# Moving one basis step behind the sums of the next layer, with VectorE's units and one norm reordered around it

## The chip, the cores and the metric

The kernel runs on one core of one Trainium2 chip. The metric is the device time of one execution in microseconds (us), the median of several runs. Where a single execution is looked at in detail it is the one that the hardware profiler recorded; its times count from the start of its span.

## The reference

A graph network of four layers works on 512 nodes with 512 features each (float32), with 16,896 edges. Each layer takes `h = relu(layernorm(x))` and adds its result to `x`.

- Layer 0 is attention with 8 heads over the edges, then a feed-forward part with two layer norms.
- Layer 1 is a linear map with PReLU, and then twice the same round: `x + segment_sum(x[src], dst)`, a product with `conv_W1`, PReLU, a product with `conv_W2`, a batch norm over the nodes (per feature), relu.
- Layer 2 is a graph convolution: `out = segment_sum(norm * (h @ W)[src], dst) + b`, then a leaky relu.
- Layer 3 is two relational convolutions. Each needs two matrices `w[r] = sum_b att[r, b] * basis[b]` from 30 bases of 512x512, for two relations and for each of the two convolutions; the basis matrices are most of what is read from memory (60 MB).

```
w = jnp.einsum('rb,bio->rio', att, basis)          # layer 3, twice
agg = jax.ops.segment_sum(x[src], dst, num_segments=n); h = x + agg   # layer 1, twice
h = _prelu(h @ conv_W1[l].T + conv_b1[l], conv_a[l]); h = h @ conv_W2[l].T + conv_b2[l]
h = (h - mean) * rsqrt(var + eps) * bn_gamma[l] + bn_beta[l]; x = relu(h)
```

## The kernel before

Nodes and features are tiles of 128 rows; `T` is 4, so a 512x512 matrix is a tile of 128 partitions by 4 by 512. The segment sums are dense products: the edges are first counted into a 512x512 matrix (`Cl` for layers 1 and 2, `Bc` for the two relations of layer 3), and a sum over edges is then a product with the counts.

The bases of layer 3 are worked into the two matrices all through the earlier layers, so that their reading from memory lies beside other work. Part of them goes over TensorE (PE) and part over VectorE:

- A **basis step** (`basis_step`) is one PE entry: four matmuls (L242) that multiply a load of up to 15 bases, cut to a few rows of each, with a small matrix of coefficients, into the PSUM bank `bas`. Two steps (in the second convolution's part three, the last with a smaller load in two pieces, L202) fill one bank; then ScalarE copies the bank to `sums` (L248) and issues a DMA to memory (L249). There is one `bas` bank, so the next bank's first step waits for that copy.
- A **unit** (`accumulate`) is a VectorE entry's quarter: one instruction (L272) that adds a coefficient times half a basis to one of the two `wrel` matrices. `advance(more, n)` issues n units; four units finish one basis.

The string `USES` gives the order in which the loads of both kinds follow each other: "P" for a basis step, "V" for a basis that VectorE uses. All loads go through one pool of four buffers (`bpool`) and are issued by SP in this order, so a load starts when an earlier entry has set its buffer free; taking an entry asks for the one three places on. Entries are numbered from 0 in the text; entry 36 is the first one behind the first batch norm's products.

The weight matrices (`w`, L160) come by DMAs that POOL issues, from a pool of three buffers; one is asked for ahead, and is issued when PE has done its last product with the buffer's former content.

The stage around the change is layer 1 and the start of layer 2. For each of the two rounds `l`:

1. the sums: 32 matmuls (L324 with four banks `acc`, in round 0 L947) into four banks; ScalarE copies banks 0 and 2 (L983) and VectorE banks 1 and 3 (L981) to `aT`;
2. four products with `conv_W1` (L324), each with a bias on ScalarE (L996) and PReLU on VectorE (L998, L999), and two units behind each;
3. four products with `conv_W2`, a bias on ScalarE (L1009), then for each of the four groups of features: the moments on VectorE (L348, L349), the root on ScalarE (L845), four small instructions on VectorE (L847 to L851), and the norm with relu on ScalarE (L852). `settle` then transposes a group on PE (L337); in round 0 it is rounded into two parts (L858, L859), in round 1 it is added to `x` (L861);
4. basis steps between the last groups.

Layer 2 starts with the moments of the four tiles of `x`, a root on ScalarE (`root`, L1039), three small instructions on VectorE (`scale`, L1042 to L1044), and the norm on ScalarE (`normed_to`, L1047), once rounded into `xn[0]` and once in full into `h`; VectorE writes the difference into `xn[1]` (L1059, L1065). Then PE runs the sums of layer 2 (`gather`, L947), with the products `gate_rows` (L809) ahead of them to fill PE's time.

Each engine runs its instructions in the order in which they stand. Most of that order is the order of the program, but a scheduler may move instructions; those that are wrapped in `on` (or in `keep_in_program_order`) stay in their order among each other. Where an `if` on a value stands around the sums (`exactly`), both branches are built and one is run.

Of the kernel before, what the change touches and what calls it, by code (L numbers as in the profile page):

```python
# [17 lines left out]
P = 128  # L18
# [12 lines left out]
RB = 4  # L31
STEPS = 2
BANKS = 8
USES = "P" * 26 + "VPVVVPPVVVPPPPVVVVPPPPPPPVVVVVVVVVVVV"
FEW = 4095
LESS = 2.0 ** -12
GW = 32
# [37 lines left out]
def gnn_kernel(ctx: ExitStack, tc: tile.TileContext, out: bass.AP, a: dict):  # L75
# [18 lines left out]
    def bank(tag):  # L94
        if tag == "sc":
            return pair()[:, 0].rearrange("p i n -> p (i n)")
        return psum[-1].tile([P, 512], F32, tag=tag, name=tag, bufs={"ao": 2, "ps": 1, "acc": 4, "pr": 2, "pg": 1}[tag])

    def ps():
        turn[1] += 1  # L100
        return bank(turn[0][turn[1] % len(turn[0])])

    def big(tag):
        return work.tile([P, T, 512], F32, tag=tag, name="big" + tag)
# [101 lines left out]
    def whole_load(l, b):  # L206
        def load():
            t = bpool.tile([P, T, 512], F32, tag="basis", name="basis")
            nc.sync.dma_start(t, nat(a[f"basis{l + 1}"][b]))
            return t  # L210
        return load
# [3 lines left out]
    ve = iter([whole_load(l, b) for l in range(2) for b in range(ONPE[l], NB)])  # L215
    bases = Stream([next(pe if u == "P" else ve) for u in USES], 0)
    bases.ahead = AHEAD
# [7 lines left out]
    def basis_step(n=1, keep=lambda ins: ins, held=None):  # L225
        for _ in range(n):
            if len(done) == len(loads):
                return
            l, n, g = loads[len(done)]
            done.append(n)  # L230
            assert USES[bases.at] == "P"
            t = bases.take()
            if g == 0:
                sums[:] = [pbas.tile([P, 512], F32, tag="bas", name="bas")]
            if g < STEPS:
                k, at = FULL * NQ, 32 - 2 * NQ * (g + 1)
                lhsT = wide[l][:k, at:at + 32]
            else:
                k = STEPS * HALF_OF * NQ
                lhsT = wide2[:k, :]  # L240
            for j in range(RB):
                tc.keep_in_program_order(nc.tensor.matmul(  # L242
                    sums[0][32 * j:32 * j + 32, :], lhsT=lhsT,
                    rhs=t[:k, j, :], start=(g == 0), stop=(g == STEPS + l - 1)))
            if g == STEPS + l - 1:
                def leave(n=n, bank=sums[0]):
                    o = spool.tile([P, 512], F32, tag="sums", name="sums")
                    keep(nc.scalar.copy(o, bank))  # L248
                    nc.scalar.dma_start(summed[l][n], o)  # L249

                if held is None:
                    leave()
                else:
                    held.append(leave)
# [9 lines left out]
    def accumulate(l, to):  # L264

        for b in range(ONPE[l], NB):
            assert USES[bases.at] == "V"
            t = bases.take()
            for r in range(2):
                at = AT1 + 2 * NB * l + NB * r + b  # L270
                for i in range(0, T, 2):
                    on(nc.vector.scalar_tensor_tensor(to[r][:, i:i + 2, :], t[:, i:i + 2, :], scal[:, at:at + 1],  # L272
                                                      to[r][:, i:i + 2, :], op0=ALU.mult, op1=ALU.add))
                    yield
# [47 lines left out]
    def product(p, pairs):  # L322
        for i, (lhsT, rhs) in enumerate(pairs):
            nc.tensor.matmul(p, lhsT=lhsT, rhs=rhs, start=(i == 0), stop=(i == len(pairs) - 1))  # L324

    def ts(i):
        return slice(i * P, (i + 1) * P)

    def on(ins):

        return tc.keep_in_program_order(ins)
# [11 lines left out]
    def stat(name, n=1):  # L343
        return small.tile([P, n], F32, name=name, bufs=3)

    def moments(mv, v, keep=lambda ins: ins):
        st = stat("st", 6)
        keep(nc.vector.bn_stats(st, v))  # L348
        keep(nc.vector.bn_aggr(mv, st))  # L349
# [340 lines left out]
    def advance(gen, n=1):  # L690
        for _ in range(n):
            next(gen, None)
# [109 lines left out]
    more = accumulate(0, wrel)  # L802
# [23 lines left out]
    def parts(hi, lo):  # L826

        return [late.tile([P, T, 512], F32R, tag=t, name=t) if t in "FG" else
                work.tile([P, T, 512], F32R, tag=t, name="big" + t) for t in (hi, lo)]
# [4 lines left out]
    def exactly(emit):  # L834

        with tc.If(made["few"] > 0) as branch:
            emit(lambda v: v, 1)
        with branch.Else():
            emit(f32, 0)

    def normed(l, h2T, m, mv):

        at = T * l + m
        sd = stat("sd")
        nc.scalar.activation(sd, mv[:, 1:2], AF.Sqrt, bias=eps)  # L845
        sg = stat("sg")
        nc.vector.reciprocal(sg, sd)  # L847
        nc.vector.tensor_mul(sg, sg, cols[:, GAM + at:GAM + at + 1])
        off = stat("off")
        nc.vector.tensor_mul(off, mv[:, 0:1], sg)  # L850
        nc.vector.tensor_sub(off, cols[:, BET + at:BET + at + 1], off)  # L851
        on(nc.scalar.activation(h2T[:, m, :], h2T[:, m, :], AF.Relu, bias=off, scale=sg))  # L852
# [84 lines left out]
    xn = parts("C", "F")  # L937
# [29 lines left out]
    for l in range(2):  # L967

        aT = big("E")
        if l:  # L970
            acc = [bank("acc") for _ in range(T)]

            def emit(f, c):
                for m in range(T):
                    product(acc[m], [(f(xn[i][:, k, ts(m)]), Clx[c][:, k, :]) for k in range(T) for i in range(2)])
            exactly(emit)
            advance(more, 3)
        for m in range(T):
            p = acc[m]
            if m % 2:  # L980
                on(nc.vector.tensor_copy(aT[:, m, :], p))  # L981
            else:
                on(nc.scalar.copy(aT[:, m, :], p))  # L983
        if l == 0:
            basis_step(1, on)
            advance(more, 4)
        else:
            advance(more, 2)
        w = weights.take()
        h1T = big("B")  # L990
        for m in range(T):
            p = ps()
            product(p, [(w[:, k, ts(m)], aT[:, k, :]) for k in range(T)])
            at = CB1 + T * l + m
            z = small.tile([P, 512], F32, name="z")
            nc.scalar.activation(z, p, AF.Identity, bias=cols[:, at:at + 1])  # L996
            u = small.tile([P, 512], F32, name="u")
            nc.vector.tensor_scalar(u, z, 0.0, scal[:, CA + l:CA + l + 1], op0=ALU.min, op1=ALU.mult)  # L998
            nc.vector.scalar_tensor_tensor(h1T[:, m, :], z, 0.0, u, op0=ALU.max, op1=ALU.add)  # L999
            advance(more, 2)  # L1000
        w = weights.take()
        h2T = big("D")
        if l == 0:
            xn = parts("A", "G")
        for m in range(T):
            p = ps()
            product(p, [(w[:, k, ts(m)], h1T[:, k, :]) for k in range(T)])
            at = CB2 + T * l + m
            on(nc.scalar.activation(h2T[:, m, :], p, AF.Identity, bias=cols[:, at:at + 1]))  # L1009
            if m:  # L1010
                normed(l, h2T, m - 1, moment)
            moment = stat("mv", 2)
            moments(moment, h2T[:, m, :])
            if m > 1:
                settle(l, h2T, m - 2, xn)
            if l and m < 3:
                advance(more)
        basis_step(1)
        normed(l, h2T, 3, moment)
        settle(l, h2T, 2, xn)  # L1020
        basis_step(3 - l)
        settle(l, h2T, 3, xn)
        if l:
            held = []
            gates = gate_rows(1, [apart.bitcast(F32).rearrange("p t n -> p (t n)")[:, N * r:N * r + N] for r in range(2)])
            next(gates)
            basis_step(1, on, held)
# [5 lines left out]
    xn = parts("C", "F")  # L1033
# [4 lines left out]
    def root(t):  # L1038
        on(nc.scalar.activation(sd4[:, t:t + 1], mv[:, t, 1:2], AF.Sqrt, bias=eps))  # L1039
# [6 lines left out]
    def normed_to(to, t):  # L1046
        on(nc.scalar.activation(to[:, t, :], x[:, t, :], AF.Relu, bias=nm[:, t:t + 1], scale=by[:, t:t + 1]))  # L1047

    for t in range(T):
        moments(mv[:, t, :], x[:, t, :], on)  # L1050
        root(t)
        if t:
            scale(t - 1)
        if t > 1:
            normed_to(xn[0], t - 2)
    scale(3)
    for t in (0, 1):
        normed_to(h, t)
# [180 lines left out]
```

## Time and profile before

| what | value |
|---|---|
| median of 3 runs | 510.31 us (509.25 to 510.54) |
| profiled execution: its own time | 511.07 us |
| profiled execution: span | 509.1 us |
| PE busy | 483.9 us (95%), 2014 instructions |
| VectorE (DVE) busy | 399.3 us (78%) |
| ScalarE (ACT) busy | 195.6 us (38%) |
| POOL busy | 37.9 us (7%) |
| chain that ended last | PE 67%, DVE 18%, ACT 8%, issue 2%, DMA 2% |
| read from memory | 88.38 MB, 184 GB/s over the span |

The profiled execution's own time is its span and 1.97 us around it. "PE" is the matmuls and "PEld" the loading of their stationary operands, which overlaps them. In a timeline each row has the start, the time that it takes, the engine, the line of the source, the operation, what it writes and reads, the count, and in brackets how long the engine stood idle before it and what ended that. In the chain each row has start, time, engine, tile, line and count; it is followed back from the last instruction. A float32 matmul shows as two matmul records, so a product of four has "x8". The DMA rows have the queue (q0 is POOL's, q1 is SP's, q10 is ScalarE's), packets, MB, and the share of the 16 DMA engines' time. In the table by stretch each engine has its busy time and count, then come the granted clock of PE, the DMA share and GB/s.

### The profile page before, as it was taken

To read this page: it belongs to the slowest core of one execution; us is meant where nothing else is said; L and a number is where in the kernel's file an instruction comes from. 1 tells how busy PE (TensorE), PEld (TensorE's weight loads), DVE (VectorE), ACT (ScalarE), POOL (GpSimd) and SP (SyncE) were. 2 spreads that over 40 slices of the span, in tenths; PEclk is the share of its full clock that TensorE was granted. 3 is DMA by queue.
4 is the path that set the end of the run, shared out by engine and by line. 5 is a ranking of instruction groups with operands and counts; after the bars stand their busy time and mean duration, and the time that the engine had idled before them with its cause. 6 is when DMAs were issued, how large, how long until landed. Compare 5 with 4: busy or idle time off the path is not lost.

```text
span 509.1 us, 5732 instructions
## 1 busy us (share of the span) xinstructions
PE 483.9 (95%) x2014; PEld 249.0 (49%) x2014; DVE 399.3 (78%) x748; ACT 195.6 (38%) x318; POOL 37.9 (7%) x81
## 2 busy tenths in 40 slices
PE   3999999999999999999999999899899999999996
PEld 2333333255564547864445444444654584446642
DVE  6847487879999779999885974797659999998611
ACT  4876779724444213223332134115624610133000
POOL 7000000100000021310040000000010100000000
PEclk9999999999999999999999999999899999999999
DMA  8999768998968499586552695866944965420011
GB/s 243 282 248 250 180 175 194 230 258 198 216 160 198 105 226 293 220 227 191 210 182 84 149 238 195 305 184 156 269 143 154 287 190 217 165 82 3 0 42 41
DMA packets 42951, 94.06 MB, mean 185 GB/s; under 512 B 2113, under 2 KB 2567, under 8 KB 42919
## 3 DMA queue, kind: packets, MB, share of 16 engines
q1 hardware_dynamic: 34682, 68.17, 49.7%
q0 software_dynamic: 5712, 21.07, 13.9%
q10 hardware_dynamic: 2525, 4.39, 2.6%
q8 instruction: 20, 0.33, 0.3%
q14 instruction: 12, 0.10, 0.1%
HBM read 88.38 MB, written 5.24 MB: 184 GB/s over the span
## 4 chain that ended last, share of the span: by engine, by line
PE 67%; DVE 18%; ACT 8%; issue 2%; DMA 2%; ACTq 0%; DVEq 0%
PE pr L324 19%; PE acc L1145 11%; PE pg L324 10%; PE acc L1111 5%; PE ps L484 4%; PE acc L947 3%; PE bas L242 3%; DVE sc L648 3%; ACT sc L649 3%; ACT hs L553 3%; DVE sc L666 3%; PE ao L562 2%; DMA basis<-in_basis 2%; DVE half L642 2%; PE ps L497 2%
## 5 line engine op out<-in xcount | busy, mean ns | idle before, releaser
L272 DVE SCALAR_TENSOR_TENSOR wrel<-basis,scal,wrel 128x1024 f32<-128x1024 f32 x60 | 74.0, 1281 | 3.9 <-DMA basis<-in_basis 3.9
L553 ACT ACTIVATE hs<-iot,key 128x512 f16<-128x512 f16 x75 | 48.8, 711 | 5.5 <-PE ao L562 4.7
L549 DVE TENSOR_SCALAR hd<-iot,key 128x32 f16<-128x32 f16 (+1 forms) x132 | 33.3, 293 | 15.4 <-PE ao L562 15.2
L242 PE MATMUL bas<-basis,wide 120*32 120x512 f32 (+1 forms) x320 | 43.5, 600 | 0.7 <-ACT sums L248 0.7
L272 DVE SCALAR_TENSOR_TENSOR w<-basis,scal,w 128x1024 f32<-128x1024 f32 x32 | 39.3, 1276 | 0.0
L562 PE MATMUL ao<-hs,hd 128*32 128x512 f16 x204 | 25.8, 397 | 2.8 <-ACT hs L553 2.6
L649 ACT ACTIVATE sc<-sc 128x2048 f32<-128x2048 f32 (+1 forms) x10 | 15.7, 1568 | 32.6 <-DVE sc L648 32.6
L484 PE MATMUL ps<-bigB,w 128*128 128x512 f32 x56 | 27.2, 615 | 0.9 <-ACT bigD L487 0.6
L324 PE MATMUL pr<-bigE,w 128*128 128x512 f32 x48 | 21.6, 596 | 1.4 <-DVE bigE L981 1.4
L1195 DVE TENSOR_TENSOR u<-acc,x 128x512 f32<-128x512 f32 (+1 forms) x5 | 2.8, 582 | 23.5 <-PE acc L1145 23.5
L324 PE MATMUL pr<-bigD,w 128*128 128x256 f32 x88 | 20.2, 380 | 0.0
L555 DVE TENSOR_SCALAR hs<-iot,key 128x512 f16<-128x512 f16 x57 | 19.2, 345 | 0.0
L648 DVE TENSOR_TENSOR sc<-sc,half 128x2048 f32<-128x2048 f32 (+1 forms) x10 | 18.6, 1862 | 0.2
L666 DVE TENSOR_TENSOR sc<-sc,rec 128x2048 f32<-128x2048 f32 x8 | 18.3, 2284 | 0.0
L633 PE MATMUL psc<-bigC,bigD 64*128 64x256 f32 x128 | 18.2, 402 | 0.0
L324 PEld LDWEIGHTS pr<-bigD,w 128*128 128x128 f32 x88 | 16.6, 190 | 3.0 <-ACT bigE L891 0.8
L356 ACT ACTIVATE sd<-mv,eps 128x1 f32<-128x1 f32 x16 | 4.7, 296 | 34.4 <-DVE mv L349 33.4
L562 PEld LDWEIGHTS <-hd 128*32 128x32 f16 x204 | 6.1, 94 | 24.2 <-issue 15.4
L324 PE MATMUL pr<-w,bigE 128*128 128x512 f32 x40 | 17.8, 592 | 0.0
L484 PEld LDWEIGHTS ps<-bigB,w 128*128 128x128 f32 x56 | 9.7, 189 | 14.9 <-issue 11.1
L664 DVE RECIPROCAL rec<-ps 128x256 f32<-128x256 f32 x8 | 14.0, 1752 | 3.7 <-PE ps L660 3.7
L635 ACT COPY sc<-psc 128x1024 f32<-128x1024 f32 x16 | 15.6, 1006 | 2.6 <-issue 1.6
(318 smaller groups left out, 960.5 us busy)
## 6 DMA issues: line engine op xcount, KB each, us to landing
basis<-in_basis SPq DMA_DIRECT2D x32, 960.0 KB
basis<-in_basis SPq DMA_DIRECT2D x23, 1024.0 KB
basis<-in_basis SPq DMA_DIRECT2D x16, 448.0 KB
summed<-sums ACTq DMA_DIRECT2D x16, 256.0 KB
w<-in_W POOLq DMA_DIRECT2D x4, 1024.0 KB, 5.6
row<-in_rows POOLq DMA_DIRECT2D x12, 256.0 KB, 7.6
wrel<-summed POOLq DMA_DIRECT2D x4, 512.0 KB, 7.5
w<-in_conv_W1T POOLq DMA_DIRECT2D x2, 1024.0 KB, 5.5
```

Source lines behind the costliest of these rows:

```text
L242: tc.keep_in_program_order(nc.tensor.matmul(sums[0][32 * j:32 * j + 32, :], lhsT=lhsT, rhs=t[:k, j, :], start=(g == 0), stop=(g == STEPS + ...
L272: on(nc.vector.scalar_tensor_tensor(to[r][:, i:i + 2, :], t[:, i:i + 2, :], scal[:, at:at + 1], to[r][:, i:i + 2, :], op0=ALU.mult, op1=AL ...
L324: nc.tensor.matmul(p, lhsT=lhsT, rhs=rhs, start=(i == 0), stop=(i == len(pairs) - 1))
L484: on(nc.tensor.matmul(p, lhsT=w[:, k, ts(m)], rhs=made["hT"][:, k, :], start=(k == 0), stop=(k == T - 1)))
L549: keep(nc.vector.tensor_scalar(hd[:, :w], iot[:, GW * groups_of[c][0]:GW * groups_of[c][0] + w], key[:, 0, c:c + 1], key[:, 2, c:c + 1], o ...
L553: keep(nc.scalar.activation(hs, iot, AF.Sign, bias=key[:, 3, c:c + 1]))
L562: keep(nc.tensor.matmul(cnt[b][GW * (g % T):GW * (g % T) + GW, :], lhsT=hd[:, at:at + GW], rhs=hs, start=(c == in_bank[g][b][0]), stop=(c ...
L648: on(nc.vector.tensor_sub(s, s, half[:, 0:1, :].to_broadcast([P, H // pieces, NH])))
L649: on(nc.scalar.activation(s, s, AF.Exp, scale=HD ** -0.5))
L666: on(nc.vector.tensor_mul(self.sc, self.sc, rec[:, None, :].to_broadcast([P, H, NH])))
L1111: nc.tensor.matmul(self.out[t], lhsT=self.hT[:, k, ts(t)], rhs=self.root[:, k, :], start=(k == 0), stop=False)
L1145: nc.tensor.matmul(self.out[t], lhsT=self.uT[r][:, k, ts(t)], rhs=wrel[r][:, k, :], start=False, stop=(r == 1 and k == T - 1))
```

## The change

In `USES` one P and one V change places, so entry 39 becomes a basis for VectorE and entry 40 a basis step. In the program the step that stood among the last three of round 0's batch norm is issued behind the sums of round 1, ahead of the first product there. In round 1, VectorE has four units in its list ahead of the copies of the sums, where it had three, and one behind them, where it had two. In layer 2, the norm of tile t-2 is issued ahead of the root of tile t and not behind the root and `scale`. Two steps remain between the third and the fourth group's `settle` in both rounds.

```diff
-USES = "P" * 26 + "VPVVVPPVVVPPPPVVVVPPPPPPPVVVVVVVVVVVV"
+USES = "P" * 26 + "VPVVVPPVVVPPPVPVVVPPPPPPPVVVVVVVVVVVV"
...
             exactly(emit)
-            advance(more, 3)
+            advance(more, 4)
         for m in range(T):
...
             basis_step(1, on)
             advance(more, 4)
         else:
-            advance(more, 2)
+            basis_step(1, on)
+            advance(more)
         w = weights.take()
...
         basis_step(1)
         normed(l, h2T, 3, moment)
         settle(l, h2T, 2, xn)
-        basis_step(3 - l)
+        basis_step(2)
         settle(l, h2T, 3, xn)
...
     for t in range(T):
         moments(mv[:, t, :], x[:, t, :], on)
+        if t > 1:
+            normed_to(xn[0], t - 2)
         root(t)
         if t:
             scale(t - 1)
-        if t > 1:
-            normed_to(xn[0], t - 2)
     scale(3)
```

## The prediction

> **What bounds the kernel now.** I read the page first: PE is busy 95% of the span, and 67% of the chain that ended last is PE's. So a change counts where PE stands still, or where work is put on PE's path. The chain, asked for the stretch around the change, says where PE stands still for something else:
>
> ```profile
> 308.81 1.04 PE bas L242 x8
> ...
> 309.87 9.96 DMA basis<-in_basis
> ...
> 319.85 2.56 DVE wrel L272 x3
> 322.41 1.03 issue
> 323.44 0.69 DVE bigE L981
> ```
>
> I number the bases by their place in USES, from 0. Entry 36's step on PE frees a buffer at 309.85; the load of entry 40, VectorE's next basis, starts into it and lands 9.96 us later; three units run, and only then the copy of the sums that PE needs. In PE's timeline the price is the wait in the last line:
>
> ```profile
> 312.09 1.92 PE L242 MATMUL bas<-basis,wide 120*32 120x512 f32 x16 [0.71 <-ACT sums L248]
> 313.95 0.66 PE L337 MATMUL pg<-ident,bigD 128*128 128x128 f32 x4
> 324.18 6.28 PE L324 MATMUL pr<-bigE,w 128*128 128x512 f32 x14 [1.43 <-DVE bigE L981]
> ```
>
> The first of these lines is entries 38 and 39, 0.96 us a step. The sums lie between the second and third, 314.36 to 321.73. The timeline of the second batch norm's tail shows the other place, a chain of latencies that ends in the first matmul of the next layer's sums (L947):
>
> ```profile
> 352.12 0.80 ACT L852 ACTIVATE bigD<-bigD,off,sg 128x512 f32<-128x512 f32 x1
> 352.97 0.66 PE L337 MATMUL pr<-ident,bigD 128*128 128x128 f32 x4
> 353.63 1.92 PE L242 MATMUL bas<-basis,wide 120*32 120x512 f32 x16
> 355.96 0.66 PE L337 MATMUL pg<-ident,bigD 128*128 128x128 f32 x4 [0.40 <-ACT bigD L852]
> ...
> 360.42 0.29 ACT L1039 ACTIVATE sds<-mvs,eps 128x1 f32<-128x1 f32 x1 [1.01 <-DVE bys L1042]
> 360.62 0.80 ACT L1047 ACTIVATE bigC<-x,nms,bys 128x512 fp32r<-128x512 f32 x1
> ...
> 361.56 1.91 PE L947 MATMUL acc<-R,bigC 128*128 128x512 f32 x4 [2.17 <-ACT bigC L1047]
> ```
>
> The third group's norm (L852, 352.12) and transposes are early, so the two basis steps fill the time in which the fourth group's norm is worked out.
>
> **The change, part by part.** Durations are of this execution: 511.07 us of its own, span 509.1, while the runs' median is 510.31; I carry the difference to the median.
>
> *The step behind the sums.* Without entry 39's step the fourth group's transposes wait only for their norm, which ends at 312.44+0.81=313.25: start 313.3 instead of 313.95. The sums keep their 7.37 us and end at 321.1. The moved step adds 0.96: PE is ready for the next product at 322.0. The step's load takes the place in SP's queue that landed at 319.82, 1.3 us ahead of need; were that cover gone, PE would wait for each us.
>
> *Four units instead of three.* VectorE's basis is now entry 39. Its load takes the place in SP's queue that was issued at about 298.8 (the second of a pair that starts at 291.84 and spans 7.36). A basis load at an idle place takes 6 to 7 us, so it is there at 306 where VectorE is free at 315.9. The 3.90 us wait on the DMA goes. Four units in a row took 4.86 us at 279.92, so they end near 320.8, and the copies of the sums (0.69) near 321.9. What is late next is PE's own step, 322.0. Sixteen matmuls at 0.858 (3.43 a product of four) end at 335.7; before, the second convolution's products began at 337.16. Gain here 1.4.
>
> *What VectorE gives back.* In the built program PE now goes through the first three products together and not one after the other, so the first is complete after eight matmuls: 322.0+8×0.858=328.9, then 0.3 to ScalarE and 0.69 there: 329.9 against 328.6. VectorE then has the same queue as before (four pairs L998 and L999, eight units), which took 14.07 from 328.64 to 342.71; now it ends at 344.0. The moments of the second batch norm are 1.25 later although PE is 1.4 earlier. PE is not stopped: its fourth right-hand side is needed after seven matmuls, at 341.8, and written at 329.9+11.75=341.7.
>
> *The tail's new order.* On ScalarE the third group's norm stood ahead of the copy of the basis sums; now it stands behind that copy, its DMA issue and the fourth group's root. On VectorE a unit (1.22) stands ahead of the fourth group's moments. The root ran at 353.98 before, held by that copy; bounds are 353.98 and 353.98 plus the 1.25 above. I take 354.0, because the 0.4 it waited and PE's lead cover most of the lag. Then norm three 0.8, transposes 0.44, two steps 1.92, and only then the fourth's transposes: 357.2, against 355.96. Loss 1.2 (bounds 1.0 and 2.4). The two steps cost nothing before, since the fourth's norm hid them; that cover is gone.
>
> *A norm ahead of a root.* L1047 started at 360.62 because it stood behind the root of group 2 (360.42); its own inputs were ready at 359.56. Gain 1.0. With the loss of 1.2, L1047 starts at 360.8, and PE could start L947 at 361.7.
>
> *The load of entry 47.* Its step is the last on PE's queue ahead of L947, so L947 waits with it. Its buffer was freed by VectorE; in the built program it is now the one that entry 44's step on PE frees. The rows:
>
> ```profile
> 350.00 0.78 SPq L202 DMA_DIRECT2D basis<-in_basis  x2
> ...
> 351.79 0.75 POOL L160 DMA_DIRECT2D w<-in_root  x1 [13.42 <-PE pg L324]
> ```
>
> So before it left ahead of POOL's weight load and had 358.33 to land by. Now PE's products end at 335.7+13.7, plus the two transposes (0.88) and 0.2 of wait: 350.5; entry 44's step ends at 351.5 and the load leaves at 351.5, while POOL's, which follows the last product, leaves at 350.4, ahead of it. What that means the DMA view shows, for the stretch 355.5 to 358.5, when the SP queue had a load waiting since 352.99:
>
> ```profile
> q0 software_dynamic: 215, 0.87, 84.8%
> q1 hardware_dynamic: 58, 0.11, 10.5%
> ```
>
> POOL's load moved from 3.5 to 6.8 us after its issue; now 353.9 to 357.2. Entry 47's 0.92 MB then go at what the SP queue got in 358 to 362, 0.79 MB in 4 us, less the tenth that slips through: to 361.4. Landing came 0.8 us behind the last bytes: 362.2. Its step 0.96: L947 starts at 363.2 and not 361.56, plus 1.65. Bounds: 361.7 if it lands in time, 364.1 if POOL's load is as slow as the 9 us that one took.
>
> [...]
>
> *Clock.* From 361.71 to 365.12 PE had half its clock, after 3.41 us in which it was busy 1.24:
>
> ```profile
> 361.71:365.12 3.41, 3.41 (x9) 2.67 (x10) 2.23 (x8) 3.40 (x6) 0.00 (x0) 0.50 1.08 229
> 358.30:361.71 3.41, 1.24 (x10) 0.34 (x10) 3.17 (x13) 1.59 (x4) 0.00 (x0) 1.00 1.01 307
> ```
>
> L947's 32 matmuls took 9.11 us instead of 32×0.228=7.3, so a halved stretch cost 1.8. The wait before L947 is no shorter after the change, so I keep 9.11. A second pause, from 351.5 to 355, is new.
>
> [...]
>
> *Sum.* L947 starts 1.65 later and keeps its length. From there the chain is PE's to the end, and the loads of entries 48 to 50 are needed at 386, so nothing takes the delay up: 511.07+1.7=512.8 for such an execution, **512.0** against the median.
>
> **Rivals.** *Entry 47 lands in time* (by 360.7). For it: 6.96 us from issue to landing before, which from 351.5 gives 358.5. Against: POOL's load is now first. Then L947 starts 0.15 to 0.9 later (F's inputs follow the last root): 510.5 to 511.2, no change that shows.
>
> *Faster.* The fourth group's moments decide the tail and come with PE's lead of 1.4, the two steps are hidden as before, the norm brings its 1.0, and entry 47 is no bound: 510.3−2.4=507.9. It decides if the third group's norm runs before 352.5. Against it: ScalarE's order is fixed and puts that norm behind the fourth's root.
>
> *The halved clock falls on the two steps too.* They and the transposes would take 2.3 more, L947 would start at 364 or later: 512.8 to 514. It decides if PE's pause behind entry 44 (3.5 us) fills as much of such a stretch as the 2.17 us ahead of L947 did.
>
> *The units still wait for their load.* Then a fourth unit lies ahead of the copy as well: plus 1.3 and more. The queue place at 298.8 speaks against it.
>
> **The numbers.** Forecast 0.46; entry 47 in time 0.28; faster 0.13; halved steps 0.11; units still waiting 0.02. A measurement of this kernel can tell about 0.3%, 1.5 us, from no change. So faster 0.13, same 0.28, slower 0.59. The range leaves out most of the faster case and the end of the clock's: 509.0 to 513.7.
>
> **What would show it.** Right: no DMA wait ahead of L272 near 316; the second convolution's products start near 335.7; the third group's L852 lies behind the fourth's root; a PE wait on basis<-in_basis just ahead of L947. Wrong: the two basis steps hidden again, or entry 47's step run before 360. A shorter L947 (under 8 us) would mean that the clock, not the order, decided.

## The result, and the profile after

The changed kernel takes 512.63 us (median of 5 runs, 511.85 to 512.80) against 510.31 for the kernel before (5 runs, 508.16 to 510.54). Over all these runs the ratio is 1.0054 with a 95% interval of 1.0031 to 1.0076 (the medians alone give 1.0045): about half a per cent slower, which is more than the noise. The profiled execution took 512.21 us of its own, 1.14 more than that of the kernel before.

The timeline of the changed kernel in the stage of the sums. From L988 on, lines are one higher than before (L998 is now L999, L1047 is L1048):

```profile
315.23 4.86 DVE L272 SCALAR_TENSOR_TENSOR wrel<-basis,scal,wrel 128x1024 f32<-128x1024 f32 x4
...
321.18 1.06 PE L242 MATMUL bas<-basis,wide 120*32 120x512 f32 x8
...
322.18 1.98 PE L324 MATMUL pr<-bigE,w 128*128 128x512 f32 x4
...
324.00 1.02 PE L324 MATMUL pg<-bigE,w 128*128 128x512 f32 x2
...
330.07 0.49 DVE L999 TENSOR_SCALAR u<-z,scal 128x512 f32<-128x512 f32 x1 [5.13 <-ACT z L997]
...
336.01 1.88 PE L324 MATMUL pr<-bigB,w 128*128 128x512 f32 x4
...
343.89 0.69 DVE L348 BATCH_NORM_STATS2 st<-bigD 128x6 f32<-128x512 f32 x1
```

The four units have no bracket: ahead of the copies VectorE no longer waits for a load. (The fifth unit, behind the copies, waits 1.68 us for its load at 323.66; VectorE has nothing else to do until 330.07.) The moved step runs at 321.18 and PE goes from it into the products without a wait; the second convolution's products start 1.15 us earlier (336.01, before 337.16). But `pr` and `pg` alternate: products are interleaved. The first PReLU comes at 330.07 instead of 328.64, and the first moments at 343.89 instead of 342.71. These lines of the kernel before are:

```profile
328.64 0.48 DVE L998 TENSOR_SCALAR u<-z,scal 128x512 f32<-128x512 f32 x1 [1.53 <-ACT z L996]
...
337.16 2.74 PE L324 MATMUL pr<-bigB,w 128*128 128x512 f32 x6
...
342.71 0.68 DVE L348 BATCH_NORM_STATS2 st<-bigD 128x6 f32<-128x512 f32 x1
```

The tail of the changed kernel, in the same view:

```profile
353.64 0.16 DVE L851 TENSOR_TENSOR off<-cols,off 128x1 f32<-128x1 f32 x1
353.73 0.29 ACT L845 ACTIVATE sd<-mv,eps 128x1 f32<-128x1 f32 x1 [1.01 <-DVE mv L349]
353.93 1.72 ACT L852 ACTIVATE bigD<-bigD,off,sg 128x512 f32<-128x512 f32 x2
...
354.78 1.11 PE L337 MATMUL pr<-ident,bigD 128*128 128x128 f32 x4 [2.71 <-ACT bigD L852]
...
355.82 3.00 PE L242 MATMUL bas<-basis,wide 120*32 120x512 f32 x16
...
358.75 0.66 PE L337 MATMUL pg<-ident,bigD 128*128 128x128 f32 x4
...
361.77 1.07 PE L242 MATMUL bas<-basis,wide 112*32 112x512 f32 x8 [0.57 <-DMA basis<-in_basis]
...
362.40 0.81 ACT L1048 ACTIVATE bigC<-x,nms,bys 128x512 fp32r<-128x512 f32 x1 [0.20 <-DVE nms L1045]
...
363.36 1.16 PE L947 MATMUL acc<-R,bigC 128*128 128x512 f32 x4 [0.53 <-ACT bigC L1048]
```

The third and the fourth group's norms (L852) now run in one go behind the fourth's root. PE waits 2.71 us for the third's, and the fourth's transposes, whose data are ready, stand behind the two steps: 358.75 instead of 355.96. The steps took 3.00 us, not 1.92. Entry 47's step waits for its load, but L947 waits for the norm, which comes later still. L947's last matmul ends at 372.05 (before 370.67).

Why the steps were slow shows in the table by stretch, cut at the edges of the slow one (busy time and count of PE, PEld, DVE, ACT, POOL; then PE's clock, DMA share, GB/s):

```profile
351.21:354.62 3.41, 0.86 (x8) 0.00 (x0) 3.07 (x11) 1.81 (x5) 0.47 (x1) 1.00 0.59 153
354.62:358.03 3.41, 3.25 (x16) 1.31 (x20) 0.85 (x2) 0.92 (x2) 0.00 (x0) 0.50 1.00 308
```

After a stretch with 0.86 us of work PE had half its clock for 3.41 us. Before, that stretch lay on L947; now it lies on the transposes and the steps, and L947 runs at full clock.

### The profile page after: what moved, and what is told of

It reads as the page before. It is cut to its first block, busy times and chain, and to the rows that moved or that the text cites. A ratio compares the mean times of both kernels' runs of the same rounds, so it can differ in the third digit from the quotient of the medians.

```text
span 510.3 us, 5733 instructions
## 1 busy us (share of the span) xinstructions
PE 484.5 (95%) x2014; PEld 247.9 (49%) x2014; DVE 398.6 (78%) x748; ACT 195.7 (38%) x318; POOL 37.6 (7%) x81
## 4 chain that ended last, share of the span: by engine, by line
PE 59%; DVE 27%; ACT 9%; issue 2%; ACTq 0%; DVEq 0%
PE pr L324 13%; PE acc L1146 11%; PE pg L324 6%; DVE wrel L272 6%; PE acc L1112 5%; PE ps L484 4%; PE bas L242 3%; DVE sc L648 3%; ACT sc L649 3%; ACT hs L553 3%; DVE sc L666 3%; PE acc L947 3%; PE ao L562 2%; DVE st L348 2%; DVE half L642 2%
## 5 line engine op out<-in xcount | busy, mean ns | idle before, releaser
L242 PE MATMUL bas<-basis,wide 120*32 120x512 f32 (+1 forms) x320 | 44.8, 615 | 1.3 <-ACT sums L248 0.7
## 6 DMA issues: line engine op xcount, KB each, us to landing
wrel<-summed POOLq DMA_DIRECT2D x4, 512.0 KB, 7.5
```

What stands on the lines that cost most here:

```text
L242: tc.keep_in_program_order(nc.tensor.matmul(sums[0][32 * j:32 * j + 32, :], lhsT=lhsT, rhs=t[:k, j, :], start=(g == 0), stop=(g == STEPS + ...
```

## The experiments

Near the change these profiles show PE's clock full, but for slow stretches of 3.41 us at half clock. Within a profile the slow stretches begin whole multiples of 3.413 us apart (43 in the kernel before, 46 in the changed one); the row of edges that this step gives is called the grid below. The theory: PE's interleaved products make VectorE late, so the third group's norm comes late, the two steps lose their cover, and PE's pause ahead of them halves the clock on them. The rival is the last step of the recorded prediction: entry 47's load alone sets L947. The first four runs have one set of runs of the kernel before as their reference (median 509.63 us), the next four another (509.9); the ratios are against these. Runs with different references are best compared by their ratios.

**The products in order.** `product` gets an argument `keep` for its matmuls:

```diff
-            product(p, [(w[:, k, ts(m)], aT[:, k, :]) for k in range(T)])
+            product(p, [...], on if l else (lambda ins: ins))
             at = CB1 + T * l + m
```

> The changed kernel, but PE runs the four products with conv_W1 of the second round one after the other (kept in program order) instead of three together. Theory (the late first product delays VectorE, the late moments push the third group's norm behind the fourth's root, and so the two basis steps stand uncovered ahead of the fourth group's transposes): the first PReLU starts near 326.6 instead of 330.07, the fourth group's transposes near 355 instead of 358.75, L947 near 360 and at full clock; 508 to 509.5 us against 512.6 of the changed kernel. Rival (the load of entry 47, late behind POOL's weight load, sets L947): the transposes are early, but entry 47's step stays at 361.7 and L947 at 362.8 or later; 511.5 or more.

Measured: 508.89 us, ratio 0.9978 (0.9963 to 0.9994). Its timeline:

```profile
326.42 0.49 DVE L999 TENSOR_SCALAR u<-z,scal 128x512 f32<-128x512 f32 x1 [1.84 <-ACT z L997]
...
352.59 1.92 PE L242 MATMUL bas<-basis,wide 120*32 120x512 f32 x16
354.94 0.66 PE L337 MATMUL pg<-ident,bigD 128*128 128x128 f32 x4 [0.43 <-ACT bigD L852]
```

One edit undoes the whole loss: the PReLU is 3.65 us earlier, the two steps are hidden again, and the transposes come at 354.94. But it sets more than PE's order: in the program built from it, ScalarE runs the third group's norm at 351.14, ahead of the copy of the basis sums (351.86) and of the fourth group's root (352.83), and not behind both. So this run shows that the interleaving is where the loss starts; what each later link costs is left to the runs below. The rival falls for this kernel, since entry 47's step ran at 357.32 without a wait. With the old order its load again left first, at 349.87, ahead of POOL's (350.43), and POOL's took 11.6 us to land. In the changed kernel POOL's left first (350.93 against 352.13) and took 6.6. The changed kernel's DMA rows for 354 to 356 are:

```profile
q0 software_dynamic: 163, 0.65, 95.7%
q1 hardware_dynamic: 6, 0.01, 1.6%
```

**The norm alone**, the last hunk of the change in the kernel before.

> The kernel before with the last part of the change alone: the norm ahead of the root. Both theories: the first norm starts 1.0 us earlier, L947 at 360.5 instead of 361.56. If the halved clock follows a fixed grid of 3.41 us and the work that PE did in the stretch before: PE is busy 2.3 instead of 1.24 us in 358.30 to 361.71, the next stretch keeps full clock, the sums of layer 2 take 7.3 to 8 us and not 9.1; 507.7 to 508.6 against 510.3. If the pause ahead of L947 halves the clock wherever it lies: L947 still takes 9.1, and the gain is the 1.0 alone: 509.3.

Measured: 508.47, ratio 0.9977 (0.9962 to 0.9991). That lies in the grid's range, but it is 1.16 less than its own reference, which was itself below 510.3; a gain of 1.0 is what the other theory has, so the time alone does not decide and the profile has to. In its profile L947 starts 3.91 us after the fourth group's addition to `x`, before 4.91: the 1.0. The clock stayed full (2.10 us of work in the stretch ahead of L947's main part):

```profile
357.85:361.26 3.41, 2.10 (x11) 1.21 (x8) 3.09 (x16) 2.95 (x6) 0.00 (x0) 1.00 1.00 284
361.26:364.67 3.41, 2.94 (x13) 2.13 (x12) 1.87 (x4) 3.41 (x6) 0.00 (x0) 1.00 1.06 232
```

L947 nevertheless took 8.7 and not 7.3: it now starts ahead of its inputs and waits for them, for `F` in the second of these lines, so most of the clock's 1.8 is not gained.

```profile
359.36 2.48 PE L947 MATMUL acc<-R,bigC 128*128 128x512 f32 x8 [1.17 <-ACT bigC L1047]
362.31 2.09 PE L947 MATMUL acc<-R,F 128*128 128x512 f32 x8 [0.47 <-DVE F L1059]
```

**The change without the norm.**

> The changed kernel without its last part: the root ahead of the norm again. Theory (the last group's chain sets L947): L947 starts 1.0 us later than in the changed kernel, at 364.4; 513.6, or up to 515 if PE's longer pause also halves the clock of the stretch from 365.1. Rival (the load of entry 47 sets L947): its step ends at 362.8 in both, so only the part of the 1.0 beyond the 0.5 that separates the two shows: 513.1 or less.

Measured: 513.65 (510.96 to 513.91), ratio 1.0063 (1.0037 to 1.0089). The first norm starts 3.97 us after the fourth addition to `x`, in the changed kernel 2.95. Entry 47's step ended at 362.5, L947 began only at 363.96: the chain, not the load, set it. A second stretch of half clock appeared, after 1.62 us of work:

```profile
361.11:364.52 3.41, 1.62 (x11) 0.69 (x12) 3.09 (x16) 1.69 (x5) 0.00 (x0) 1.00 1.02 215
364.52:367.93 3.41, 3.41 (x9) 2.46 (x8) 1.89 (x6) 3.41 (x6) 0.00 (x0) 0.50 1.06 232
```

**The two steps behind the last transposes**, all other engines' order kept:

```diff
-        basis_step(2)
+        basis_step(0 if l else 2)
         settle(l, h2T, 3, xn)
         if l:
-            held = []
+            held = []; basis_step(2)
```

> The changed kernel with the two basis steps issued behind the fourth group's transposes in round 1; every other engine's order is the same. Theory (the two uncovered steps are the loss): the transposes move from 358.75 to about 355.8, the first norm of layer 2 from 362.4 to about 359.5; then the load of entry 47, which lands near 361.6, is the bound, so L947 starts at 362.7 with all its inputs there and takes 7.3: a gain of about 1.9, 510.7. Rival (the two steps are hidden anyway, entry 47's load alone sets the time): L947 as above but no shorter, a gain of 0.5, 512.1.

Measured: 511.01 (509.98 to 512.25), ratio 1.0027 (1.0013 to 1.0042). Its timeline:

```profile
354.66 0.66 PE L337 MATMUL pg<-ident,bigD 128*128 128x128 f32 x4 [0.26 <-ACT bigD L852]
355.24 1.92 PE L242 MATMUL bas<-basis,wide 120*32 120x512 f32 x16
...
361.01 1.06 PE L242 MATMUL bas<-basis,wide 112*32 112x512 f32 x8 [1.86 <-DMA basis<-in_basis]
362.01 2.11 PE L947 MATMUL acc<-R,bigC 128*128 128x512 f32 x8
```

The ratio is 0.0027 below the changed kernel's, some 1.4 us, where the theory had 1.9 and the rival 0.5; the two intervals overlap, so its size is not well known. With the transposes early, entry 47's load is what L947 waits for: the prediction's wait is real, it only ended a little before another one in the changed kernel. The pause of 2.72 us was still there, yet the steps ran at full clock. Counted back by 45 times 3.413 us from the slow stretch that begins at 506.38, near the program's end, an edge of the grid lay at 352.78 in this execution (an estimate): the pause was split over two stretches with 1.66 and 2.19 us of work.

**The pause filled**, with three products into a bank that is not read:

```diff
-        basis_step(1)
+        basis_step(1); more_pe = [on(nc.tensor.matmul(q, lhsT=ident, rhs=h1T[:, 0, :], start=True, stop=True)) for q in [ps()] for _ in range(3)] if l else []
         normed(l, h2T, 3, moment)
```

> The changed kernel with three products into a bank that nobody reads (2.6 us of PE), in PE's pause behind entry 44's step. Theory (the clock is halved for a stretch of 3.41 us on a fixed grid when PE was idle for most of the stretch before): the stretch from 351.5 is now busy, the two basis steps take 1.92 instead of 3.00, the fourth group's transposes come at 357.2 instead of 358.75, L947 at 362.8 with its inputs there; 510.9 to 511.4. Rival (the lower clock has nothing to do with PE's pause, or the three products only push the transposes back): no gain, 512.6 or more.

Measured: 510.77 (509.74 to 514.33), ratio 1.0026 (1.0008 to 1.0044); the median is just under the theory's range: more work, less time. Here too the interval overlaps that of the changed kernel, and not every execution gained: three of the eleven, with a granted clock of 0.993 to 0.995, took 512.48 to 514.33. Where their slow stretches lay is not recorded. In the profiled execution the steps have their full clock, and the wait for entry 47 is back:

```profile
351.67 2.84 PE L1019 MATMUL pr<-bigB,ident 128*128 128x512 f32 x6
...
355.05 1.92 PE L242 MATMUL bas<-basis,wide 120*32 120x512 f32 x16
356.90 0.66 PE L337 MATMUL pr<-ident,bigD 128*128 128x128 f32 x4
...
361.51 1.06 PE L242 MATMUL bas<-basis,wide 112*32 112x512 f32 x8 [2.16 <-DMA basis<-in_basis]
```

**POOL's load held back as well**, in the kernel with the steps last. Ahead of the load of `root2`, POOL copies a column of `x` into its tile, which waits for the third group (`late` is true for `root2` alone):

```diff
-            t = wpool.tile([P, T, 512], F32, tag="w", name="w")
+            t = wpool.tile([P, T, 512], F32, tag="w", name="w"); late and nc.gpsimd.tensor_copy(t[:, 0, 0:1], x[:, 0, 300:301])
```

> The run with the two steps last, in which PE waited 1.86 us for entry 47; here POOL's load of the last root's weights is also held back, by a copy of one column that waits for the third group's addition to x (near 354.5). Theory (the load that was issued first shuts the other out): entry 47 lands near 357 to 358 and not 361, PE does not wait for it, L947 starts near 359.3 with the gaps of its norm chain, 509.3 to 509.9 against 511.0. Rival (the load takes nine us by itself): PE waits for entry 47 as before, 511.0.

Measured: 510.57 (508.09 to 511.84), ratio 1.0003 (0.9987 to 1.0018). The wait for entry 47 is gone (its step at 362.19 has none), but in the profiled execution a slow stretch (a clock of 0.51 from 356.00 to 359.41) fell on the steps, which took 2.87 us. The median missed the range:

```profile
357.41 2.87 PE L242 MATMUL bas<-basis,wide 120*32 120x512 f32 x16
```

What the grid does to the median can be read from the granted clock, which is on record for every execution as the mean over its span; by estimate one slow stretch takes about 0.003 off it (half of 3.41 in 510). Five executions of this run at 1.000 took 508.09 to 509.44 us, at or below the theory's range, and seven at 0.992 to 0.997 took 510.55 to 511.84. Without the norm, one execution at 1.000 took 510.96 and six at 0.992 to 0.997 took 513.58 to 513.91. With the steps last alone the groups lie closer: three at 0.998 and 0.999 took 509.98 to 510.70, nine at 0.992 to 0.997 took 510.50 to 512.25. All five of the changed kernel are at 0.993 to 0.997. So among executions at or near full clock those with the load held back are some 1.6 us shorter on average; whether anything else varied along with the clock is not recorded.

**The stall at the sums, without moving the step.** The kernel before with the norm ahead and, by the same kind of copy from `xn[1]`, POOL's load of `l2_W` (layer 2's weights) behind entry 40's:

> The kernel before with the norm ahead of the root, and with POOL's load of layer 2's weights held back until the fourth group of the first batch norm is rounded (near 315.5), so that it is issued after the load of entry 40. Theory (the stall at the sums is that load being shut out by POOL's): entry 40 lands near 316.5 instead of 318.6 to 319.9, PE never waits for the copies of the sums; 507.4 to 508.5, the gain over the norm alone (508.47) being what the stall costs in a usual execution, 0 to 1.4. Rival (entry 40 is late by itself): it lands at 318.6 or later, 508.5.

Measured: 507.86 (507.11 to 508.27), ratio 0.9955 (0.9942 to 0.9968), faster than the kernel before and than the changed one.

```profile
316.03 3.68 DVE L272 SCALAR_TENSOR_TENSOR wrel<-basis,scal,wrel 128x1024 f32<-128x1024 f32 x3
...
321.83 4.45 PE L324 MATMUL pr<-bigE,w 128*128 128x512 f32 x10
```

POOL's load now leaves at 317.66. Entry 40 is there when VectorE is free, where with the norm alone VectorE waited 2.53 us for it, and PE goes straight on. In this execution the wait that the change removes is gone by the order of two loads as well, with the step left where it was.

**The kernel before once more**, for its profile.

> The kernel before once more, for its profile alone: how long PE waits for the copies of the sums in another execution. The prediction took 1.43 us for every execution; the run with the norm alone, whose stage is the same, showed 0.05. Theory: the wait varies with when the load of entry 40 lands, between 0 and 1.5.

Measured in its one execution: 510.91 us, with a wait of 1.60 at the same place, the first line below. So of three executions of this stage two had 1.43 and 1.60, and that of the run with the norm alone 0.05, where entry 40 landed 8.6 us after its issue and not 10 (the second line).

```profile
324.11 6.28 PE L324 MATMUL pr<-bigE,w 128*128 128x512 f32 x14 [1.60 <-DVE bigE L981]
...
318.65 3.68 DVE L272 SCALAR_TENSOR_TENSOR wrel<-basis,scal,wrel 128x1024 f32<-128x1024 f32 x3 [2.53 <-DMA basis<-in_basis]
```

## Why the prediction was right, and which terms were not

**The step behind the sums, four units: right in this execution, too large as a rule.** The products began at 322.18 (forecast 322.0), the second convolution's at 336.01 (335.7). But the 1.4 is the stall of one profile. Without a stall the move costs: 0.96 for the step, less the 0.6 by which the transposes come earlier. The products in order have this part and the norm and no late tail, and stand at 0.9978; the norm alone stands at 0.9977. No gain of this part shows; no run has it by itself.

**What VectorE gives back: right.** Forecast 329.9 and 344.0, measured 330.07 and 343.89; the run with the products in order, where the first PReLU comes at 326.42, shows the cause.

**The tail's new order: right in its place, incomplete in its cause.** L852 ran at 353.93 (forecast 354.0, with the 0.2 that the root ahead of it takes left out; the root came at 353.73). The prediction blamed ScalarE's order; VectorE's was as late, since the fourth's moments and an addition to `x` stand within the third's small chain, whose L851 ended at 353.80. The transposes were forecast for 357.2 and came at 358.75. The missing 1.5 is the rival that the prediction gave 0.11 and left out of its sum: 0.45 on the transposes and 1.08 on the steps, at half clock.

**The norm ahead of a root: right**, 1.0 by both runs that isolate it.

**The load of entry 47: right in its landing, wrong in its rank.** The forecast had it at 362.2; PE's wait for it ended at 361.77. Two errors met in that: SP's queue had the engines from about 356 (67.4% of their time from 356 to 357) and not from 357.2, and the load then took longer than the 5.0 of the forecast. Its step ended at 362.84, but the first norm only at 363.21, so the chain won by 0.4. That L947 nevertheless began at 363.36, close to the forecast's 363.2, is in part luck: with full clock on the transposes and steps the first norm would have ended near 361.7 (363.21 less 1.53, an estimate), and L947 would have begun behind the load's step, near 362.8. Where the chain is early the load is the bound (waits of 1.86 and 2.16). POOL's queue was ahead as forecast: SP's load had been issued at 352.13, and from 354 to 356 its queue had 1.6% of the engines' time and POOL's 95.7%.

**The clock: wrong.** The prediction kept 9.11 us for L947; it took 8.69, with no halved stretch but with gaps for its inputs. The slow stretch fell on the transposes and the steps here (354.62 to 358.03) and on L947 before (361.71 to 365.12). The prediction kept the pattern of one execution.

**The sum.** L947 began 1.80 later (forecast 1.65) and was 0.42 shorter (forecast 0): by 372 us the kernel is 1.37 behind, and at its end 1.14 against the forecast's 1.7. The forecast was 512.8 for such an execution and 512.0 for the median; measured were 512.21 and 512.63, so the 0.8 that was carried from one to the other belonged to that one profile of before. The total came out in part by luck. The half clock on the transposes and steps, which the sum left out, cost 1.5 and hid most of the wait that the sum had charged to the load; and L947 was 0.42 shorter than the sum had it.

## What to carry to other kernels

Before moving work to fill a wait, look at which of two transfers left first; to swap their order may be enough. Here the swap with the norm stands at 0.9955 and the move with the norm, products in order, at 0.9978; their intervals just overlap. Look in the built order whether products that were one after the other become interleaved, because the first result then can come late even if the last comes early (here the first PReLU came 1.43 later, the second convolution's products 1.15 earlier). And take the size of a stall (1.43, 1.60 and 0.05 in three executions here), or of a slow stretch of the clock, from several executions.

## What the runs showed of the hardware

- Slow stretches of PE's clock lay on a grid within an execution: they began at 361.71 and 508.48 in the kernel before (43 times 3.413 apart), at 354.28 and 364.52 in the change without the norm (3 times). Between executions the grid shifted: in the kernel before once more the slow stretch began at 361.20. With the steps last, PE ran the same order in two runs, and the two steps took 1.92 us in one and 2.87 in the other.
- Near the change half clock followed six stretches in five runs, with 0.69 to 1.62 us of work in 3.41. None followed a stretch with 1.66 or more; the 1.66 (49%) is that with the steps last.
- The queue whose load was issued first had most of the DMA engines' time in two stretches: from 354 to 356 in the changed kernel POOL's had 95.7% and SP's 1.6% (issued at 350.93 and 352.13), and from 352 to 354 with the products in order SP's had 93.6% and POOL's 3.5% (issued at 349.87 and 350.43). POOL's load landed 6.6 and 6.4 us after its issue where it left first (changed kernel, steps last), 9.0 and 9.1 us where SP's had a lead of 1.8 (norm alone, kernel before), and 11.6 us where SP's had a lead of 0.56 (products in order).
